# A two-layer spectral and cosine convolution on one core: sums over q as plain transposes with the DFT at their eviction, and one of the shifted inputs copied on chip

## The chip, the cores and the metric

The kernel runs on one core of a Trainium2 chip. The metric is the device time of one execution in microseconds; the time before is 19604.93 us, the median of three (19579.76 to 19606.49). The profiled execution took 19570.94 us.

## The reference

The input x is 4 images of 512 x 512 positions with 16 channels, in fp32. Two residual layers follow each other:

```python
H_truncated = rfft2(b) / rfft2(a)            # b: numerators, a: denominators, 9 x 9 taps
H = rfft2(irfft2(H_truncated), s=(1024, 1024))
X = rfft2(gn(x), s=(1024, 1024))
Y = einsum('...hwi,ijhw->...hwj', X, h0 + H)
x = x + irfft2(Y)[..., :512, :512, :]
# second layer: a 3 x 3 cosine convolution with arccos and tanh of norms
x = x + cosine_conv(gn(x))
```

gn is a group normalization with 8 groups. What matters here is the line with einsum: at each of 513 x 1024 frequencies, 16 input channels are mixed to 16 output channels by a complex 16 x 16 matrix, for four images.

## The kernel before, in words

The work has four phases, one after another: the filter's transform (filter_phase, results to g_d in DRAM), the input's transform along one axis (forward_phase, to x_d), the convolution (conv_phase, from g_d and x_d to y_d), and the inverse transform with the second layer (last_phase). Only conv_phase and its tables are touched by the change.

conv_phase (line 657) goes over 513 rows, one for each frequency of the axis that is already transformed, the first two of which are halves of one stored row. For each row it transforms x along the other axis, multiplies by the filter, and transforms back. The loop is a software pipeline written by hand: `step(n)` (line 849) works on five rows at once, in four quarters k = 0 to 3. A scheduler then orders each engine's instructions by readiness in its own estimate, so an instruction can stand earlier in an engine's stream than in the source. These are the parts, by the tile names that the profile uses:

- `load_x` (705), `turn_x` (716), `x_part` (724): row n+2 of x is transformed by four matmuls with dfs_n, a table turned by this row's own phase (`own`, one column for each row). The result px (PSUM, two banks) is evicted into slot 0 of the tile xe, in two halves.
- `x_late` (739): xe has eight slots, t = 0 to 7. Slot t is slot 0 moved by t places along the spatial axis, that is by 16 t partitions. What moves in from the far end is the same data times a phase; GpSimd computes it as xl, with four products xu (line 753), one product xl (754) and one sum (755). Two stores (746) put slot 0 and xl one below the other into xf_d in DRAM.
- `load_xe` (760): in the next step one load on the sync engine's queue reads seven overlapping windows of xf_d into slots 1 to 7, 3.5 MiB.
- `load_g` (693), `g_part` (768): the filter of row n+1 is loaded to g and transformed with dg: 32 matmuls, pg, evicted to gh.
- `mix` (785): the product at each of 128 frequencies f, 128 matmuls of 32 columns, pm, evicted to yf.
- `over_q` (805): one half of the transform back, over q, for row n-1. yf holds, for a time slot t, partitions (q, c, j) by columns (g, x): q is one of 4 frequency classes, c real or imaginary, j the channel. A matmul with the table iq does two things at once: it puts (g, x) on the partitions, and it sums over q with a phase for each s0 of 4. Sixteen matmuls per row, in groups of four: pz, evicted to z.
- `over_g` (821): the other half, over the 32 values of g, for row n-2: eight matmuls with ig, py, evicted to yo and stored to y_d by GpSimd.

`evict` (line 686) sends copies out of PSUM to VectorE and ScalarE in turn. PSUM has eight banks: three for pg, two for pm, and three, with the tag "full", shared by px, pz and py. xe has three buffers, g, x, gh, yf, z and yo have two, xu and xl have one. The sync engine's queue issues the loads of xe, g and x; GpSimd's queue issues the stores to xf_d and y_d. The step that a reader needs most is the order:

```python
        if row(3):
            load_x(n + 3)
        if row(2):
            load_g(n + 2)
        if row(1):
            load_xe(n + 1)
        for k in range(4):
            ... # mix(n), g_part(n + 1), over_q(n - 1): a quarter each
            if row(2) and k == 0:
                for m in range(B):
                    x_part(n + 2, m)
                x_late(n + 2)
```

Of the kernel before, what the change touches and what calls it, by code (L numbers as in the profile page):

```python
# [40 lines left out]
F32 = mybir.dt.float32  # L41
AF = mybir.ActivationFunctionType
ALU = mybir.AluOpType
# [3 lines left out]
P = 128  # L47
N = 512
B = 4
C = 16  # L50
S = 64
F = 128
# [4 lines left out]
XF = F * 2 * B  # L57
# [12 lines left out]
def constants():  # L70

    c = {}
# [31 lines left out]
    for r in range(33):  # L104
        full = np.zeros((2, S), complex)
# [4 lines left out]
        for part in range(2):  # L110
# [6 lines left out]
            else:  # L117
                v = -(sig.real @ np.sin(f_all))
# [21 lines left out]
    c["own"] = np.tile(own.reshape(-1), (P, 1))  # L140
# [4 lines left out]
    def turn(n, of):  # L145
        a = 2 * np.pi * (n % of) / of
        return np.cos(a), np.sin(a)

    f, sb = np.arange(F), np.arange(S)
    d = np.zeros((2, S, F, 2))  # L150
    co, si = turn(np.outer(sb, f), F)
    d[0, :, :, 0], d[0, :, :, 1] = co, -si
    d[1, :, :, 0], d[1, :, :, 1] = si, co
    c["dfs"] = np.stack([d, np.stack([d[..., 1], -d[..., 0]], -1)], 2).reshape(P, -1)
    co, si = turn(f, F)
    c["late"] = np.tile(np.concatenate([co, si, -si]), (P, 1))

    q1 = np.zeros((4, 2, C, 4, 2, C))
    for q in range(4):
        for cg in range(2):  # L160
            for s0 in range(4):
                co, si = turn(np.array(cg + q * (s0 - 31.5)), 4)
                for j in range(C):
                    q1[q, cg, j, s0, 0, j], q1[q, cg, j, s0, 1, j] = co, si
    c["iq"] = q1.reshape(P, P)

    gg, s1 = np.arange(32), np.arange(16)
    ig = np.zeros((32, 2, 2, 4, 2, 2, 2, 16))
    for s0 in range(4):
        for cx in range(2):  # L170
            for c2 in range(2):
                n = gg[:, None] * (s0 - 31.5) + 4 * gg[:, None] * s1[None, :] + 32 * (cx + c2)
                co, si = turn(n, F)
                for b2 in range(2):
                    ig[:, cx, b2, s0, c2, 0, b2, :] = co / F
                    ig[:, cx, b2, s0, c2, 1, b2, :] = si / F
# [480 lines left out]
def conv_phase(tc, cst, g_d, x_d, y_d):  # L657
    nc = tc.nc
    with ExitStack() as ctx:
# [12 lines left out]
        own = load_const(nc, cp, cst, "own").rearrange("p (v n) -> p v n", v=2)  # L672
        dg = load_const(nc, cp, cst, "dg")
        iq = load_const(nc, cp, cst, "iq")
# [10 lines left out]

        def evict(dst, src):
            flip[0] += 1
            if flip[0] % 2:
                nc.vector.tensor_copy(dst, src)  # L689
            else:  # L690
                nc.scalar.copy(dst, src)  # L691
# [23 lines left out]

        def turn_x(n):

            t = xlp.tile([P, 2 * F], F32, name="turn")
            nc.scalar.activation(t, dfs[:, 1], AF.Identity, scale=own[:, 1, n : n + 1])
            m = xlp.tile([P, 2 * F], F32, name="dfs_n", bufs=2)  # L720
            nc.vector.scalar_tensor_tensor(m, dfs[:, 0], own[:, 0, n : n + 1], t, ALU.mult, ALU.add)
            state["dfs", n] = m

        def x_part(n, b):
# [14 lines left out]
        def x_late(n):  # L739

            xe = state["xe", n][:, 0]
            fl = xe.rearrange("p f h c k -> p f (h c k)")

            def store(half, t):
                at = slice(C, P) if half == 0 else slice(0, P - C)
                nc.gpsimd.dma_start(out=xf_d[n % 4][half * P :, :][at], in_=t[at].rearrange("p f x -> p (f x)"))

            store(0, fl)
            xl = xlp.tile([P, F, 2, 2, 2], F32, name="xl")
            u = xlp.tile([P, F, 2, 2, 2], F32, name="xu")  # L750
            for c in range(2):
                for h in range(2):
                    nc.gpsimd.tensor_mul(u[:, :, h, c], xe[:, :, h, 1 - c], bc(late[:, 1 + c], 2, [P, F, 2]))  # L753
            nc.gpsimd.tensor_mul(xl.rearrange("p f h c k -> p f (h c k)"), fl, bc(late[:, 0], 2, [P, F, 8]))
            nc.gpsimd.tensor_add(xl.rearrange("p f h c k -> p (f h c k)"),
                                 xl.rearrange("p f h c k -> p (f h c k)"),
                                 u.rearrange("p f h c k -> p (f h c k)"))
            store(1, xl.rearrange("p f h c k -> p f (h c k)"))

        def load_xe(n):  # L760
            src = xf_d[n % 4]
            nc.sync.dma_start(
                out=state["xe", n][:, 1:].rearrange("p t f h c k -> p t (f h c k)"),
                in_=bass.AP(tensor=src.tensor, offset=src.offset + C * XF,
                            ap=[[XF, P], [C * XF, 7], [1, XF]]),
            )

        def g_part(n, j):

# [34 lines left out]

        def over_q(n, t):

            y, k = state["y", n], t // 4
            if t % 4 == 0:
                state["pz"] = ps_f.tile([P, 4, P], F32, name="pz", tag="full")
            pz = state["pz"]  # L810
            at = 2 * (2 * k + 1 - t % 4 // 2) + t % 2
            nc.tensor.matmul(pz[:, t % 4], y[:, at].rearrange("p g x -> p (g x)"), iq, start=True, stop=True)  # L812
            if t == 3:
                state["z", n] = yp.tile([P, 8, 2, 8, C], F32, name="z")
            if t % 4 == 3:
                evict(state["z", n][:, 6 - 2 * k : 8 - 2 * k].rearrange("p t h x j -> p (t h x j)"),
                      pz.rearrange("p t x -> p (t x)"))
            if t == 15:
                del state["y", n]

        def over_g(n, k):

            rc, r, plane = rows[n]
            if k == 0:
                state["py"] = ps_f.tile([P, 2, 2, 8, C], F32, name="py", tag="full")
            z, py = state["z", n], state["py"]
            odd, c2 = k // 2, k % 2
            for half in range(2):
                s0 = 2 * half + odd
                nc.tensor.matmul(  # L830
                    py[64 * half : 64 * half + 64, odd], ig[:, s0, c2],
                    z[:, :, :, 2 * s0 + c2, :].rearrange("p t h j -> p h t j"),
                    start=(c2 == 0), stop=(c2 == 1),
                )
            if k < 3:
                return
            del state["z", n]
            yo = yop.tile([P, 4 * P], F32, name="yo")
            evict(yo.rearrange("p (x j t) -> p x j t", x=4, j=C), py.rearrange("p o h t j -> p (o h) j t"))
            if plane is None:  # L840
                nc.gpsimd.dma_start(out=dram(y_d[rc], r, 0, [4 * P, P], [1, 4 * P]), in_=yo)
            else:
                for half in range(2):
                    nc.gpsimd.dma_start(
                        out=dram(y_d[rc], r, (64 * half + 32 * plane) * 4 * P, [4 * P, 32], [1, 4 * P]),
                        in_=yo[64 * half : 64 * half + 32],
                    )

        def step(n):


            def row(k):
                return 0 <= n + k < n_rows
# [8 lines that stand above are left out]
                if row(0):  # L862
                    for g in range(8):
                        mix(n, 8 * k + g)
                if row(1):
                    for j in range(4):
                        g_part(n + 1, 4 * k + j)
                if row(-1):
                    for t in range(4):
                        over_q(n - 1, 4 * k + t)  # L870
                if row(2) and k == 0:
                    for m in range(B):
                        x_part(n + 2, m)
# [452 lines left out]
```

## Time and profile before

The span of the profiled execution, 19569.2 us, divides by the first and last matmul of `mix`:

| stretch, us | phase | length | PE busy | DVE busy | ACT busy | POOL busy | DMA share | GB/s |
|---|---|---|---|---|---|---|---|---|
| 0 to 6980 | filter, then forward | 6980 | 6493.88 | 4826.35 | 3411.00 | 4448.79 | 0.55 | 157 |
| 6980 to 16570 | convolution | 9590 | 8810.89 | 3771.26 | 3061.07 | 4464.24 | 0.88 | 331 |
| 16570 to 19569 | last | 2999 | 2698.54 | 1644.63 | 1553.13 | 1353.38 | 0.52 | 181 |

PE is TensorE's matmul, DVE is VectorE, ACT is ScalarE, POOL is GpSimd and SP the sync engine. In lines of the profile, `pz<-c_iq,yf` is the tile written and the tiles read; a name after `<-` in brackets or after an idle time is what released the instruction. A letter q behind an engine is its instruction queue: SPq issues transfers. An fp32 matmul appears as two instructions. The costliest groups of the convolution, per instruction: pg 288 ns (32832 of them), pm 221 ns (131328), pz 295 ns (16416) on TensorE; 692 ns for a 512-column eviction on VectorE and 586 ns on ScalarE; 718 ns for one xu on GpSimd. These durations include the time in TensorE's pipeline, so that the spacing of their starts, not their sum, tells how long they occupy it.

### The profile page before, as it was taken

Reading aid. Unit: us, or ns where it says so; the run is one execution under the profiler, and the core shown is the slowest. Engines: PE = TensorE matmul, PEld = TensorE weight load, DVE = VectorE, ACT = ScalarE, POOL = GpSimd, SP = SyncE. Lnnn points to the kernel's source line nnn. Section 1 sums busy time; section 2 is a strip of 40 time slices with the busy share of each in tenths; the row PEclk is TensorE's granted clock in tenths of the full one; section 3 lists DMA queues with packets and bytes.
Section 4 is the critical chain, followed back from the end, with each engine's and each line's share of the span. In section 5 each row is a group of like instructions: output and inputs, shape, how many; then the busy total and the mean of one; then the engine's idle time right before and its main releaser. Section 6 shows DMA issues by size and latency. Waiting matters only on the chain. (4 is left out here: it accounts for less than half of the span.)

```text
span 19569.2 us, 539471 instructions
## 1 busy us (share of the span) xinstructions
PE 18003.3 (92%) x235228; PEld 13539.4 (69%) x235228; DVE 10242.2 (52%) x16010; ACT 8025.2 (41%) x14536; POOL 10266.4 (52%) x11419
## 2 busy tenths in 40 slices
PE   8899999999989989999999999999999998988999
PEld 5455555555544467777777777777777776877888
DVE  8877777777753333333333333333333333246656
ACT  4455555555542223333333333333333332106777
POOL 7677777777741134444444444444444443026655
PEclk8899999999999999999999999999999999998999
DMA  3655554555566578888888888888888887796421
GB/s 104 202 149 150 148 142 140 150 148 148 148 195 187 177 288 333 331 332 330 334 331 334 329 334 332 333 331 332 331 334 332 334 331 292 270 325 223 140 74 61
DMA packets 2974924, 4812.42 MB, mean 246 GB/s; under 512 B 109107, under 2 KB 2076813, under 8 KB 2865679
## 3 DMA queue, kind: packets, MB, share of 16 engines
q1 hardware_dynamic: 2742366, 4037.77, 60.1%
q0 software_dynamic: 174896, 605.89, 7.8%
q10 hardware_dynamic: 55296, 134.24, 2.0%
q8 instruction: 1849, 30.29, 0.6%
q14 instruction: 517, 4.23, 0.1%
HBM read 3300.13 MB, written 1477.31 MB: 244 GB/s over the span
## 5 line engine op out<-in xcount | busy, mean ns | idle before, releaser
L753 POOL TENSOR_TENSOR xu<-xe,c_late 128x256 f32<-128x256 f32 x2052 | 1427.6, 718 | 4162.1 <-DVE xe L689 2218.4
L776 PE MATMUL pg<-c_dg,g 64*128 64x128 f32 x32832 | 2477.5, 288 | 437.1 <-DMA g<-g_d 293.1
L689 DVE COPY gh<-pg 128x512 f32<-128x512 f32 x2052 | 1419.4, 692 | 2417.0 <-PE pg L776 2412.6
L792 PE MATMUL pm<-xe,gh 128*32 128x64 f32 x131328 | 2375.8, 221 | 330.6 <-issue 282.2
L792 PEld LDWEIGHTS pm<-xe,gh 128*32 128x32 f32 x131328 | 1983.7, 110 | 877.8 <-issue 725.5
L379 PE MATMUL pg<-c_dinv,sp 128*128 128x256 f32 x8192 | 2278.1, 426 | 295.7 <-ACT st L384 193.1
L776 PEld LDWEIGHTS pg<-c_dg,g 64*128 64x128 f32 x32832 | 2063.4, 190 | 671.7 <-issue 396.6
L812 PE MATMUL pz<-c_iq,yf 128*128 128x128 f32 x16416 | 2465.7, 295 | 27.2 <-issue 21.2
L379 PEld LDWEIGHTS pg<-c_dinv,sp 128*128 128x128 f32 x8192 | 1611.2, 207 | 941.7 <-ACT st L384 217.5
L812 PEld LDWEIGHTS pz<-c_iq,yf 128*128 128x128 f32 x16416 | 2059.4, 197 | 287.7 <-issue 41.2
L691 ACT COPY gh<-pg 128x512 f32<-128x512 f32 x2052 | 1201.7, 586 | 2475.3 <-PE pg L776 2475.2
L355 DVE RECIPROCAL dn<-dn 128x256 f32<-128x256 f32 x1024 | 1790.3, 1748 | 778.8 <-POOL dn L348 778.8
L424 PE MATMUL pt<-ev_in,c_todd 128*128 128x512 f32 x4096 | 1980.2, 609 | 48.5 <-DMA ev_in<-g_d 25.7
L342 ACT COPY ab<-pab 128x512 f32<-128x512 f32 x2048 | 1103.5, 591 | 1136.1 <-POOL m L362 312.3
L689 DVE COPY yf<-pm 128x512 f32<-128x512 f32 x1029 | 711.8, 692 | 1606.4 <-PE pm L792 1584.4
L384 ACT COPY st<-pg 128x256 f32<-128x256 f32 x2048 | 1070.5, 622 | 1019.1 <-PE pg L379 638.3
L1179 PE MATMUL pc<-l_band,xn 128*128 128x160 f32 (+3 forms) x9024 | 1369.3, 308 | 63.3 <-DVE e_o L1226 62.4
L357 POOL TENSOR_TENSOR x<-ab,ab 128x256 f32<-128x256 f32 x1024 | 876.1, 856 | 945.7 <-ACT ab L342 919.4
L1179 PEld LDWEIGHTS pc<-l_band,xn 128*128 128x128 f32 x9024 | 1215.1, 197 | 220.6 <-issue 145.1
L336 PEld LDWEIGHTS pab<-c_e,u 18*128 18x128 f32 x8192 | 722.9, 188 | 809.7 <-ACT st L384 454.2
L424 PEld LDWEIGHTS pt<-ev_in,c_todd 128*128 128x128 f32 x4096 | 812.1, 199 | 676.6 <-issue 520.0
L691 ACT COPY yf<-pm 128x512 f32<-128x512 f32 x1023 | 593.9, 581 | 1578.1 <-PE pm L792 1578.1
(185 smaller groups left out, 28650.5 us busy)
## 6 DMA issues: line engine op xcount, KB each, us to landing
xe<-xf_d SPq DMA_DIRECT2D x513, 3584.0 KB, 14.3
g<-g_d SPq DMA_DIRECT2D x511, 1024.0 KB, 17.0
g_d<-st SPq DMA_DIRECT2D x64, 4096.0 KB, 34.5
ev_in<-g_d SPq DMA_DIRECT2D x1024, 256.0 KB, 4.7
g_d<-ot SPq DMA_DIRECT2D x1024, 256.0 KB, 2.7
xf_d<-xe POOLq DMA_DIRECT2D x513, 448.0 KB, 8.4
xf_d<-xl POOLq DMA_DIRECT2D x513, 448.0 KB, 7.0
x_d<-xo SPq DMA_DIRECT2D x128, 1024.0 KB, 5.4
```

The costliest lines, as they stand in the source:

```text
L342: nc.scalar.copy(w["ab"][n], pp[n])
L355: nc.vector.reciprocal(w["dn"], w["dn"])
L379: nc.tensor.matmul(pg[:, k].rearrange("p a x -> p (a x)"), w["sp"][:, k, c, :], dinv[:, 2 * kp + k, c, :], start=(c == 0), stop=(c == 1),)
L384: nc.scalar.copy(st[a][:, :, i].rearrange("p (q k x) -> p k q x", q=2, k=4)[:, 2 * kp : 2 * kp + 2], pg[:, :, a].rearrange("p k (q x) -> p ...
L424: nc.tensor.matmul(pt, todd[:, c, kc, hh * P : hh * P + P], ev[:, kc, c], start=(kc == 0), stop=(kc == 1),)
L689: nc.vector.tensor_copy(dst, src)
L691: nc.scalar.copy(dst, src)
L753: nc.gpsimd.tensor_mul(u[:, :, h, c], xe[:, :, h, 1 - c], bc(late[:, 1 + c], 2, [P, F, 2]))
L776: nc.tensor.matmul(pg[c][:, j % 4], g[half, j], dg[half], start=True, stop=True)
L792: nc.tensor.matmul(pm[32 * q : 32 * q + 32, g % 8], gh[:, f].rearrange("p c j -> p (c j)"), xe[:, :, f].rearrange("p t h c k -> p t (h c k ...
L812: nc.tensor.matmul(pz[:, t % 4], y[:, at].rearrange("p g x -> p (g x)"), iq, start=True, stop=True)
L1179: nc.tensor.matmul(pc[:, lo:hi, :].rearrange("p w j -> p (w j)"), xns[q][:, h * P + dh : h * P + dh + P], bands[dh][:, o : o + hi - lo, :] ...
```

## The change

It does three things in conv_phase.

First, the sums over q no longer are matmuls with the table iq. `over_q` transposes yf with the identity, which is one instruction instead of two, and the four-point DFT over q is done while pz is evicted: ScalarE copies one half of pz to a tile zq, and VectorE makes sums and differences of it with the other half in five operations, the last ones into z. For odd s0 a product with the imaginary unit is left; GpSimd does it for the whole row with one difference, into a new tile zd, and one sum, in place in z. `over_g` then reads z or zd. For this to be a plain DFT, the offset of 31.5 places is moved from the tables iq and ig into the table dfs.

Second, slot 4 of xe, the input moved by 64 partitions, is not loaded any more. Its lower half is the upper half of slot 0, and its upper half the lower half of xl; ScalarE copies both on chip (`half_shift`). The load of xe becomes two loads of three slots each.

Third, to make room, the table own is loaded in nine pieces as needed, and one eviction in three goes to VectorE, the others to ScalarE, since VectorE has the new work.

```diff
@@ constants
-    co, si = turn(np.outer(sb, f), F)
+    co, si = turn(np.outer(sb + 31.5, f), F)
...
-                n = gg[:, None] * (s0 - 31.5) + 4 * gg[:, None] * s1[None, :] + 32 * (cx + c2)
+                n = gg[:, None] * s0 + 4 * gg[:, None] * s1[None, :] + 32 * (cx + c2)
@@ evict
-            if flip[0] % 2:
+            if flip[0] % 3 == 0:
                 nc.vector.tensor_copy(dst, src)
@@ turn_x
+            for k in range(2) if n == 0 else [n // 64 + 1] if n % 64 == 0 else []:
+                if k < 9:
+                    state["own", k] = xlp.tile([P, 2, 64], F32, name="own", bufs=3)
...
@@ after x_late
+        def half_shift(n, half):
+
+            dst, src = ((slice(0, 64), state["xe", n][64:, 0]), (slice(64, P), state["xl"][:64]))[half]
+            nc.scalar.copy(state["xe", n][dst, 4].rearrange("p f h c k -> p (f h c k)"),
+                           src.rearrange("p f h c k -> p (f h c k)"))
@@ load_xe
-            nc.sync.dma_start(
-                out=state["xe", n][:, 1:].rearrange("p t f h c k -> p t (f h c k)"),
-                in_=bass.AP(tensor=src.tensor, offset=src.offset + C * XF,
-                            ap=[[XF, P], [C * XF, 7], [1, XF]]),
-            )
+            for t in (1, 5):
+                nc.sync.dma_start(
+                    out=state["xe", n][:, t : t + 3].rearrange("p t f h c k -> p t (f h c k)"),
+                    in_=bass.AP(tensor=src.tensor, offset=src.offset + t * C * XF,
+                                ap=[[XF, P], [C * XF, 3], [1, XF]]),
+                )
@@ over_q
-            nc.tensor.matmul(pz[:, t % 4], y[:, at].rearrange("p g x -> p (g x)"), iq, start=True, stop=True)
+            nc.tensor.transpose(pz[:, t % 4].rearrange("p v q x -> p (v q x)"),
+                                y[:, at].rearrange("p g x -> p (g x)"), ident)
...
-                evict(state["z", n][:, 6 - 2 * k : 8 - 2 * k].rearrange("p t h x j -> p (t h x j)"),
-                      pz.rearrange("p t x -> p (t x)"))
+                z = state["z", n][:, 12 - 4 * k : 16 - 4 * k].rearrange("p t (v q) j -> p t v (q j)", v=4)
+                lo = xlp.tile([P, 4, 2, 2 * C], F32, name="zq", bufs=2)
+                nc.scalar.copy(lo, pz[:, :, 0])
+                nc.vector.tensor_sub(z[:, :, 2:4], lo, pz[:, :, 1])
+                nc.vector.tensor_add(lo[:, :, 0], lo[:, :, 0], pz[:, :, 1, 0])
+                nc.vector.tensor_add(pz[:, :, 1, 1], lo[:, :, 1], pz[:, :, 1, 1])
+                nc.vector.tensor_add(z[:, :, 0], lo[:, :, 0], pz[:, :, 1, 1])
+                nc.vector.tensor_sub(z[:, :, 1], lo[:, :, 0], pz[:, :, 1, 1])
             if t == 15:
+
+                z, d = state["z", n], xlp.tile([P, 16, 2, C], F32, name="zd")
+                nc.gpsimd.tensor_sub(d, z[:, :, 4:6], z[:, :, 6:8][:, :, ::-1])
+
+                nc.gpsimd.tensor_add(z[:, :, 4:6], z[:, :, 4:6], z[:, :, 6:8][:, :, ::-1])
@@ over_g
+                if s0 % 2 == 0:
+                    zs = z[:, :, s0 + c2]
+                elif s0 == 1:
+                    zs = (d[:, :, 0], z[:, :, 5])[c2]
+                else:
+                    zs = (z[:, :, 4], d[:, :, 1])[c2]
@@ step, in quarter k
+                if row(2) and k >= 2:
+                    half_shift(n + 2, k - 2)
```

More of the change, by code (lines that the diff above doesn't have):

```diff
@@ L139, in constants @@
     own = np.stack([np.r_[1, -1, np.cos(own)], np.r_[0, 0, np.sin(own)]])
-    c["own"] = np.tile(own.reshape(-1), (P, 1))
+    own = np.pad(own, ((0, 0), (0, 9 * 64 - own.shape[1]))).reshape(2, 9, 64)
+    c["own"] = np.tile(own.transpose(1, 0, 2).reshape(-1), (P, 1))
     inv = fwd * np.where(f > 0, 2.0, 1.0)[:, None] / (2 * N)
@@ L156, in constants @@
     c["late"] = np.tile(np.concatenate([co, si, -si]), (P, 1))
[L158 to L165, printed above, removed]
     gg, s1 = np.arange(32), np.arange(16)
@@ L671, in conv_phase @@
         dfs = load_const(nc, cp, cst, "dfs").rearrange("p (v n) -> p v n", v=2)
-        own = load_const(nc, cp, cst, "own").rearrange("p (v n) -> p v n", v=2)
         dg = load_const(nc, cp, cst, "dg")
-        iq = load_const(nc, cp, cst, "iq")
+        ident = load_const(nc, cp, cst, "ident")
         ig = load_const(nc, cp, cst, "ig").rearrange("p (s c n) -> p s c n", s=4, c=2)
@@ L716, in turn_x @@
         def turn_x(n):
+            for k in range(2) if n == 0 else [n // 64 + 1] if n % 64 == 0 else []:
+                if k < 9:
+                    state["own", k] = xlp.tile([P, 2, 64], F32, name="own", bufs=3)
+                    nc.sync.dma_start(
+                        out=state["own", k].rearrange("p v n -> p (v n)"), in_=cst["own"][:, 128 * k : 128 * k + 128]
+                    )
+            own, at = state["own", n // 64], slice(n % 64, n % 64 + 1)
             t = xlp.tile([P, 2 * F], F32, name="turn")
-            nc.scalar.activation(t, dfs[:, 1], AF.Identity, scale=own[:, 1, n : n + 1])
+            nc.scalar.activation(t, dfs[:, 1], AF.Identity, scale=own[:, 1, at])
             m = xlp.tile([P, 2 * F], F32, name="dfs_n", bufs=2)
-            nc.vector.scalar_tensor_tensor(m, dfs[:, 0], own[:, 0, n : n + 1], t, ALU.mult, ALU.add)
+            nc.vector.scalar_tensor_tensor(m, dfs[:, 0], own[:, 0, at], t, ALU.mult, ALU.add)
             state["dfs", n] = m
@@ L758, in x_late @@
             store(1, xl.rearrange("p f h c k -> p f (h c k)"))
+            state["xl"] = xl
+        def half_shift(n, half):
+            dst, src = ((slice(0, 64), state["xe", n][64:, 0]), (slice(64, P), state["xl"][:64]))[half]
+            nc.scalar.copy(state["xe", n][dst, 4].rearrange("p f h c k -> p (f h c k)"),
+                           src.rearrange("p f h c k -> p (f h c k)"))
         def load_xe(n):
             src = xf_d[n % 4]
-            nc.sync.dma_start(
-                out=state["xe", n][:, 1:].rearrange("p t f h c k -> p t (f h c k)"),
-                in_=bass.AP(tensor=src.tensor, offset=src.offset + C * XF,
-                            ap=[[XF, P], [C * XF, 7], [1, XF]]),
-            )
+            for t in (1, 5):
+                nc.sync.dma_start(
+                    out=state["xe", n][:, t : t + 3].rearrange("p t f h c k -> p t (f h c k)"),
+                    in_=bass.AP(tensor=src.tensor, offset=src.offset + t * C * XF,
+                                ap=[[XF, P], [C * XF, 3], [1, XF]]),
+                )
         def g_part(n, j):
@@ L808, in over_q @@
             if t % 4 == 0:
-                state["pz"] = ps_f.tile([P, 4, P], F32, name="pz", tag="full")
+                state["pz"] = ps_f.tile([P, 4, 2, 2, 2 * C], F32, name="pz", tag="full")
             pz = state["pz"]
             at = 2 * (2 * k + 1 - t % 4 // 2) + t % 2
-            nc.tensor.matmul(pz[:, t % 4], y[:, at].rearrange("p g x -> p (g x)"), iq, start=True, stop=True)
+            nc.tensor.transpose(pz[:, t % 4].rearrange("p v q x -> p (v q x)"),
+                                y[:, at].rearrange("p g x -> p (g x)"), ident)
             if t == 3:
-                state["z", n] = yp.tile([P, 8, 2, 8, C], F32, name="z")
+                state["z", n] = yp.tile([P, 16, 8, C], F32, name="z")
             if t % 4 == 3:
-                evict(state["z", n][:, 6 - 2 * k : 8 - 2 * k].rearrange("p t h x j -> p (t h x j)"),
-                      pz.rearrange("p t x -> p (t x)"))
+                z = state["z", n][:, 12 - 4 * k : 16 - 4 * k].rearrange("p t (v q) j -> p t v (q j)", v=4)
[6 more added lines that the diff above has]
+                nc.vector.tensor_sub(z[:, :, 1], lo[:, :, 0], pz[:, :, 1, 1])
             if t == 15:
+                z, d = state["z", n], xlp.tile([P, 16, 2, C], F32, name="zd")
+                nc.gpsimd.tensor_sub(d, z[:, :, 4:6], z[:, :, 6:8][:, :, ::-1])
+                nc.gpsimd.tensor_add(z[:, :, 4:6], z[:, :, 4:6], z[:, :, 6:8][:, :, ::-1])
+                state["zd", n] = d
                 del state["y", n]
@@ L825, in over_g @@
                 state["py"] = ps_f.tile([P, 2, 2, 8, C], F32, name="py", tag="full")
-            z, py = state["z", n], state["py"]
+            z, d, py = state["z", n], state["zd", n], state["py"]
             odd, c2 = k // 2, k % 2
@@ L829, in over_g @@
                 s0 = 2 * half + odd
+                if s0 % 2 == 0:
[4 more added lines that the diff above has]
+                    zs = (z[:, :, 4], d[:, :, 1])[c2]
                 nc.tensor.matmul(
                     py[64 * half : 64 * half + 64, odd], ig[:, s0, c2],
-                    z[:, :, :, 2 * s0 + c2, :].rearrange("p t h j -> p h t j"),
+                    zs.rearrange("p (t h) j -> p h t j", h=2),
                     start=(c2 == 0), stop=(c2 == 1),
@@ L836, in over_g @@
                 return
-            del state["z", n]
+            del state["z", n], state["zd", n]
             yo = yop.tile([P, 4 * P], F32, name="yo")
```

## The prediction

> **What bounds the kernel now.** First the page's busy line and its forty slices.
>
> ```profile
> PE 18003.3 (92%) x235228; PEld 13539.4 (69%) x235228; DVE 10242.2 (52%) x16010; ACT 8025.2 (41%) x14536; POOL 10266.4 (52%) x11419
> ...
> DMA  3655554555566578888888888888888887796421
> ```
>
> TensorE at 92% looks like the bound, but the convolution, slices 14 to 33, also keeps the DMA engines at 88%. By the view of line 792 its first matmul starts at 6982.3 us and its last at 16568.6: 9586.3 us for 512 steps, 18.72 us a step. Next, the waits between 9000 and 10000 us (53.4 steps).
>
> ```profile
> POOL xu L753 <- DVE xe L689: 233.5, 27, 13.0
> ...
> PE pg L776 <- DMA g<-g_d: 32.2, 27, 2.6
> ```
>
> The DMA queue's own waits in the same stretch:
>
> ```profile
> SPq L762 <- DMA xf_d<-xe: 445.7, 46, 14.0
> SPq L762 <- DMA xf_d<-xl: 301.0, 52, 14.9
> ```
>
> The queue that reloads xe waits 14 us of every step for the two stores to xf_d. TensorE's wait for g is small but comes once per step. The DMA view of 9500 to 9600 us (2.5 us a slice) shows one hole per step:
>
> ```profile
> DMA  9939999993699999728999994499999918999996
> ```
>
> The timeline gives the order. TensorE:
>
> ```profile
> 9561.89 1.16 PE L776 MATMUL pg<-c_dg,g 64*128 64x128 f32 x16 [0.82 <-DMA g<-g_d]
> 9562.99 1.16 PE L812 MATMUL pz<-c_iq,yf 128*128 128x128 f32 x8
> 9563.98 1.89 PE L732 MATMUL px<-dfs_n,x 128*128 128x256 f32 x8
> ```
>
> GpSimd:
>
> ```profile
> 9565.89 1.53 POOL L753 TENSOR_TENSOR xu<-xe,c_late 128x256 f32<-128x256 f32 x2 [7.98 <-DVE xe L689]
> ...
> 9573.95 0.58 POOL L746 DMA_DIRECT2D xf_d<-xl  x1 [0.29 <-POOL xl L755]
> ```
>
> The queue:
>
> ```profile
> 9543.35 0.37 SPq L762 DMA_DIRECT2D xe<-xf_d  x1
> ...
> 9581.62 0.37 SPq L762 DMA_DIRECT2D xe<-xf_d  x1
> ```
>
> This is a ring. The load of xe, with g behind it, is issued at 9543.35; g lets TensorE go on at 9561.89 (18.54 us later); px starts at 9563.98 (2.09); its eviction releases GpSimd at 9565.89 (1.91); the second store is issued at 9573.95 (8.06); it lands and the reload of two steps later goes out at 9581.62 (7.67). The sum, 38.27 us, is two steps. Averaged over the timeline's steps from 7500 to 16000 us whose landings are recorded, the terms are 17.62 (xe issue to g landed), 2.93, 1.98, 8.07 and 6.69, with 0.08 to the issue: 37.37 us, 18.69 a step against 18.72. So the kernel is bound by this ring of transfers. TensorE without waits needs, by the spacing of the starts in the same timeline, four times 1.03 (pm) + 1.09 (pg) + 1.07 (pz), with px 1.82 and py 1.88: 16.5 us. It waits 2.2 us a step although it counts as busy.
>
> [...]
>
> **The change part by part.**
>
> *Transposes.* 16 fp32 matmuls a step are two instructions each (16416 is 32 per step); a group of four takes 1.09 us from start to start, 0.99 ahead of px. The transposes of line 1101 and line 613 are one instruction each, and four take 0.45 us in the timeline of the forward phase (6006.84 to 6007.29). I take 0.50 for the switch. TensorE saves 4 x 0.57 = 2.3 us: 14.2 us a step of its own. Of this only the group between pg and px, 0.5 us, lies on the ring.
>
> *Less to load, in two pieces around g.* Seven slots of 512 KB become six, 3 ahead of g and 3 behind (the built program has this order; x goes ahead of them). The last wanted is now the second half of xe, after 4.0 MiB instead of 4.5. Loading g takes 17.62 - 14.46 (xe's average landing) = 3.2 us for 1.0 MiB, so 0.5 MiB less is 1.6: 16.0 us from issue to the last landing. But xe is wanted by the first pm, g only by the pg behind it: 1.03 us more follow the landing.
>
> *Landing to px.* 1.03 (pm) + 1.09 (pg) + 0.50 (pz) + 0.1 to start = 2.7 us (2.93 before).
>
> *px to GpSimd.* ScalarE now always takes the first half of xe. Where it did before, 9507.76 to 9509.53, it took 1.77 us; the copy of pz ahead of it (0.4 us) is over by then.
>
> *GpSimd to the second store.* 8.07 us, plus a wait: VectorE's half of xe, which the first store needs, stands behind five new operations. [...] It starts 0.8 after px does, so VectorE's xe is over at 3.3, and GpSimd would have been ready at 1.77 + 1.35 = 3.1. I add 0.3: 8.4 us. If an operation costs 400 ns, it is 0.8 us.
>
> *The two new GpSimd operations* (512 elements each) stand ahead of xu. Line 1217 takes 1.28 us for 512, so 2.6 together. They are free only if they end before xe is ready. Their start depends on the last pz group of the step, and this on ScalarE's copies of half of xe: the built program puts the second of these, which waits for xl, behind the second pz copy of the step and not at the end. It will hold ScalarE's queue: behind it stand a yf, a gh, a pz copy and yo, and TensorE's fourth pg group waits for that gh's buffer. Counted from xu's start: xl ready 8.1; copy 1.1 (509 ns for 256 elements at line 719 and 710 for 512 at line 1205 give 0.79 ns an element; 617 for 512 at line 1196 give 1.02 for 1024): 9.2; yf and gh at 0.5 each: 10.2; pg 1.1 and pz 0.7: 12.0; pz copy 0.5; VectorE 1.75; GpSimd 2.6: 16.9 us, when xu of the next step could start. That is a second ring of one step, 16.9 us, with 16.2 to 18.3 for slower or quicker pieces. Below the first, it hides.
>
> *Stores.* 6.69 us before, of which about 5.7 lay beside the loads and 1.0 after them. The loads end sooner, so the store has the engines alone longer: between 4.4 (the least landing in the view of line 746 from 9000 to 10000 us) and 6.7; I take 6.3.
>
> *Others, at nothing.* ScalarE has 10 evictions, 4 copies of pz, 2 half copies and one turn: 10 x 0.585 + 4 x 0.42 + 2 x 1.02 + 0.51 = 10.1 us a step, VectorE 5 x 0.69 + 4 x 1.75 + 0.85 = 11.3, GpSimd 8.7 + 2.6 = 11.3: all under 17, and the rings hold what of them is on the path. The own table comes in 9 small loads, two pieces ahead. over_g reads other strides of the same bytes. The other phases are the same.
>
> Sum: 16.0 + 2.7 + 1.8 + 8.4 + 6.3 + 0.1 = 35.3 us in two steps, 17.65 a step; I take 17.7 because the second ring is close. Saved: (18.72 - 17.7) x 512 = 520 us, 19604.9 - 520 = 19085, said as 19090. With the bounds: store 4.4 and no added wait gives 16.5, where the second ring holds it at 16.9 or more; store 7.2, the added wait 0.8, landing 16.6 gives 18.3.
>
> **The rivals.** *TensorE was the bound.* For it: 92%. Against it: the ring's sum and the hole. Then the saving is 2.3 x 512 = 1180: 18430 us. *Half the gain is eaten*: the second ring at 18.3 sets the step, 215 us saved, 19390. *Slower*: with z operations of 0.4 us (2.1 a group)[...], and a store no faster, the zd pair ends 2 us after xe is ready, is added to the first ring once per step, and TensorE, which now waits about 3.5 us a step, drops its clock as it did at 9542.51 (pg 2.03 us instead of 1.16), right on the ring. Ring one gets 35.3 + 0.4 + 2 + 1.6 (half clock on a part of pm, pg, px) = 39.3, 19.65 a step: 480 us more, 20080. For it: three engines' queues are newly tied together. Against it: each has 6 us of slack a step.
>
> **How the numbers follow.** Forecast, 18700 to 19350: 0.55. Half eaten, 19350 to 19565: 0.17. TensorE bound or a much quicker store, under 18700: 0.08. No change within 0.2% (39 us): 0.06. Slower: 0.14. Faster is 0.55 + 0.17 + 0.08 = 0.80. The range 18700 to 19600 leaves out 0.08 below and about 0.13 above.
>
> **What would show it.** Right: about 17.7 us a step; TensorE's wait once a step is for xe and not for g; the queue still waits for xf_d; one hole per step in the DMA line; ScalarE waiting on GpSimd's xl some 3 us a step; pz's rows halved in count. Wrong: xu released by zd instead of xe (the second ring rules); TensorE without any wait (it was the bound); a granted clock in the convolution clearly under its 0.98; a DMA line without holes.

## The result, and the profile after

The kernel after takes 19064.0 us (median of 4 runs, 19048.82 to 19086.82) against 19605.71 us before (4 runs, 19579.76 to 19609.93): ratio 0.9727, 95% interval 0.9711 to 0.9744, or 542 us less. The page of the kernel after, its busy line and the DMA row of its forty slices:

```profile
PE 17293.1 (91%) x227020; PEld 12605.2 (66%) x227020; DVE 11398.8 (60%) x23961; ACT 9747.4 (51%) x17871; POOL 11564.3 (61%) x12445
...
DMA  3755455555557668888888888888888887796321
```

Neither line tells that anything became faster: TensorE is at 91% instead of 92%, the DMA engines are as full as before (0.87 of the convolution against 0.88). Only the convolution is shorter. Its first pm matmul (line 799 now) starts at 6990.1 us, its last at 16042.0: 9051.9 us for 512 steps, **17.68 us a step** against 18.72. The phases ahead of it and behind it take as long as before, within 10 us each.

The waits of the kernel after between 9000 and 10000 us, 56.6 steps (total us, times, longest):

```profile
ACT xe L763 <- POOL xl L754: 208.1, 57, 6.5
...
POOL xu L752 <- ACT xe L683: 93.6, 56, 6.9
```

ScalarE waits for GpSimd's xl 3.7 us a step, as it must for the second half copy. GpSimd's xu still waits for xe, not for zd: the new GpSimd operations are over in time. TensorE's own waits in the same stretch:

```profile
PE pm L799 <- issue: 41.6, 45, 2.9
PE pg L783 <- issue: 18.0, 13, 3.2
PE pg L783 <- ACT gh L683: 16.1, 21, 2.5
PE pm L799 <- DMA xe<-xf_d: 14.0, 10, 2.9
```

Its wait for g is gone and one for xe has come, but only in 10 steps of 57. The largest item, "issue", is a stop for which the profile shows no cause; the experiments will come back to it. The DMA queue's waits, and the DMA row from 9500 to 9600 us (2.5 us a slice), which still has one hole per step:

```profile
SPq L769 <- DMA xf_d<-xl: 724.7, 56, 14.5
```

```profile
DMA  9995799999539999974998995599999539999964
```

The timeline of the kernel after, one turn of the ring (start, length, engine, line; the bracket is the idle time ahead and who ended it):

```profile
9509.52 0.37 SPq L769 DMA_DIRECT2D xe<-xf_d  x1
...
9530.33 1.89 PE L731 MATMUL px<-dfs_n,x 128*128 128x256 f32 x8
...
9532.07 1.37 POOL L752 TENSOR_TENSOR xu<-xe,c_late 128x256 f32<-128x256 f32 x2 [1.28 <-ACT xe L683]
...
9540.15 0.58 POOL L745 DMA_DIRECT2D xf_d<-xl  x1 [0.29 <-POOL xl L754]
...
9545.05 0.37 SPq L769 DMA_DIRECT2D xe<-xf_d  x1
```

From load to load it is 35.53 us, two steps, as before but 2.7 us shorter. Averaged over the 190 turns between 7500 and 15500 us whose landings are recorded:

| term, us | predicted | after |
|---|---|---|
| issue of xe to its last landing | 16.0 | 15.78 |
| landing to px | 2.7 | 4.22 |
| px to xu | 1.8 | 1.75 |
| xu to the second store | 8.4 | 8.13 |
| store's landing | 6.3 | 5.31 |
| to the next issue | 0.1 | 0.16 |
| sum, two steps | 35.3 | 35.36 |

The sum is met to 0.1 us, but that alone shows little: the terms run from one issue to the issue two steps later, so in any kernel they add up to two steps, whatever binds it. A ring binds only where each piece starts as soon as the one before it ends. Two terms are off by 1.5 and 1.0 us against each other, and "landing to px" is 1.5 us over its tenth percentile (2.75), which is what it takes when nothing else holds px. With 2.75 the ring would need 33.9 us, 16.9 a step. So the ring has slack there, and something else is about as slow. The experiments look for it.

### The profile page after: what moved, and what is told of

Read it like the earlier page. It is cut to its first block, busy times and chain, and to the rows that moved or that the text cites. A ratio compares the mean times of both kernels' runs of the same rounds, so it can differ in the third digit from the quotient of the medians.

```text
span 19052.5 us, 536690 instructions
## 1 busy us (share of the span) xinstructions
PE 17293.1 (91%) x227020; PEld 12605.2 (66%) x227020; DVE 11398.8 (60%) x23961; ACT 9747.4 (51%) x17871; POOL 11564.3 (61%) x12445
## 5 line engine op out<-in xcount | busy, mean ns | idle before, releaser
L783 PE MATMUL pg<-c_dg,g 64*128 64x128 f32 x32832 | 2842.9, 291 | 320.9 <-ACT gh L683 159.5
L783 PEld LDWEIGHTS pg<-c_dg,g 64*128 64x128 f32 x32832 | 2283.2, 190 | 662.7 <-issue 262.5
L828 DVE TENSOR_TENSOR z<-zq,pz 128x256 f32<-128x256 f32 x2052 | 862.0, 420 | 2617.2 <-ACT zq L827 2534.6
L683 ACT COPY yf<-pm 128x512 f32<-128x512 f32 x2046 | 1210.5, 592 | 919.0 <-PE pm L799 904.3
L763 ACT COPY xe<-xl 64x1024 f32<-64x1024 f32 x513 | 538.8, 1050 | 1877.0 <-POOL xl L754 1877.0
L820 PE MATMUL pz<-c_ident,yf 128*128 128x128 f32 x8208 | 1378.2, 291 | 27.2 <-issue 25.4
```

What stands on the lines that cost most here:

```text
L783: nc.tensor.matmul(pg[c][:, j % 4], g[half, j], dg[half], start=True, stop=True)
L820: nc.tensor.transpose(pz[:, t % 4].rearrange("p v q x -> p (v q x)"), y[:, at].rearrange("p g x -> p (g x)"), ident)
```

## The experiments

The theory is the prediction's: a ring of fixed terms through the transfers sets the step. The rivals are that the one-step ring through ScalarE's half copy does, that the bytes to be moved do, or that TensorE does. Ratios are to the kernel before, measured beside each.

### One part of the change alone

transposes_only keeps the change but for the copies; shift_only has only the copies.

Of transposes_only, against after:

```diff
-            for t in (1, 5):
-                nc.sync.dma_start(
-                    out=state["xe", n][:, t : t + 3].rearrange("p t f h c k -> p t (f h c k)"),
...
+            nc.sync.dma_start(
+                out=state["xe", n][:, 1:].rearrange("p t f h c k -> p t (f h c k)"),
...
-                if row(2) and k >= 2:
-                    half_shift(n + 2, k - 2)
```

shift_only makes the same edit the other way round in the kernel before, with `half_shift` added.

> The kernel after with its transposes and its new evictions, but the seven slots of xe loaded in one piece and no copies on the chip. If the ring of transfers sets the step, it loses only the 0.6 us of one pz group in two steps: 18.4 us a step, 160 us under the kernel before. If TensorE alone was the bound, 2.3 us a step: 1180 us under it.

> The kernel before with six slots loaded in two pieces and the two half copies, but the sums over q still as fp32 matmuls. If the ring of transfers alone sets the step, 35.3 + 0.6 us in two steps, 17.95 a step: 400 us under the kernel before. If TensorE, with its stops under load, needs about 18.4 us a step with the old matmuls (where the kernel before without the GpSimd sum ended), it can't fall below that: 160 us under. If the bytes loaded set it, 8% of 18.7 us: 700 us under.

transposes_only: 19624.14 us, ratio 1.0016 (1.0010 to 1.0023). shift_only: 19182.33 us, ratio 0.9794 (0.9780 to 0.9809), 416 us less. So the transposes alone bring nothing, the copies alone three quarters of the 542 us that both bring together: the transposes are worth some 120 us, but only once the copies are there.

The first is a miss of 0.3 us a step for the ring. Why it gained nothing, its waits and timeline show:

```profile
PE pg L782 <- DMA g<-g_d: 79.5, 34, 5.6
```

```profile
9531.42 0.76 PE L782 MATMUL pg<-c_dg,g 64*128 64x128 f32 x2 [5.59 <-DMA g<-g_d]
...
9532.12 1.93 PE L798 MATMUL pm<-xe,gh 128*32 128x64 f32 x64
...
9533.98 2.07 PE L782 MATMUL pg<-c_dg,g 64*128 64x128 f32 x14
...
9535.98 1.11 PE L819 MATMUL pz<-c_ident,yf 128*128 128x128 f32 x4
```

TensorE, quicker by the transposes, now waits 79.5 us instead of 32.2 for g. But the way from g's landing to px, which is on the ring, takes 4.23 us on average against 3.15 in the kernel before. Two things lengthen it. First, TensorE's instructions stand in another order: between the pg that waits for g and px there is now a group of pm, as these lines show, where the kernel before had pg and pz alone. Even the tenth percentile of this way is 3.13 us instead of 2.22, though pz is shorter. Second, after the idle time of 5.59 us TensorE runs at half its clock (granted 0.50 over these lines): pm 1.93 us instead of 1.10, pg 2.07 instead of 1.16, pz 1.11 instead of 0.66. Of the 266 steps between 7500 and 15500 us whose landing is recorded, the clock stays over 0.98 between g and px in 150, and the way takes 3.52 us; in 112 it is under 0.9, and the way takes 5.08. Together they eat what the shorter pz saves there.

shift_only agrees with the fixed ring (17.95 a step; measured 17.92). Yet its TensorE doesn't wait for data at all; its stops are of this kind:

```profile
9525.44 0.92 PE L784 MATMUL pg<-c_dg,g 64*128 64x128 f32 x5 [2.32 <-issue]
9526.29 2.07 PE L820 MATMUL pz<-c_iq,yf 128*128 128x128 f32 x8
```

So its agreement is no proof of the ring: TensorE itself set this one (a table below has 17.0 us busy and 0.8 us of stops in its 17.9). After this stop of 2.32 us pz takes 2.07 us instead of 1.16, nearly twice as long.

### Shortening GpSimd's part of the ring

before_no_sum leaves out the sum of xl and xu in the kernel before (its output misses that term).

```diff
-            nc.gpsimd.tensor_add(xl.rearrange("p f h c k -> p f (h c k)"),
-                                 xl.rearrange("p f h c k -> p f (h c k)"),
-                                 u.rearrange("p f h c k -> p f (h c k)"))
```

> The kernel before, with GpSimd's sum into xl (line 755, 2.36 us a step) left out, so that the late half of the input is only its first product. Nothing of TensorE's work changes. If the kernel before is bound by its ring of transfers, which goes through GpSimd once in two steps, the ring's 37.4 us become 37.4 - 2.4 = 35.0, 17.5 a step instead of 18.72: 1.2 x 512 = 610 us less, about 18990 us. If TensorE at 92% were the bound, the time would stay at 19600.

It took 19434.27 us, ratio 0.9916 (0.9896 to 0.9935). The way from xu to the second store fell from 8.03 to 5.60 us, 1.2 us a step, but the step only by 0.26 (18.72 to 18.46). The store's landing stretched from 6.72 to 7.83 us and the way from g to px from 3.15 to 3.47. TensorE's waits in it:

```profile
PE pm L789 <- issue: 33.8, 45, 1.8
PE pg L773 <- issue: 22.8, 21, 2.2
PE pg L773 <- DMA g<-g_d: 14.6, 16, 2.0
```

The wait for g has halved, and "issue" is the greater part. So the ring held the kernel before, but something else, by these waits TensorE, stood only some 0.3 us a step behind it.

### ScalarE's wait, and the product on VectorE

hs_end places the half copy of xl behind the step's last pz copy; hs_end_dve also moves the product of xl from GpSimd to VectorE.

```diff
-                nc.scalar.copy(lo, pz[:, :, 0])
+                state["last"] = nc.scalar.copy(lo, pz[:, :, 0])
...
-                if row(2) and k >= 2:
-                    half_shift(n + 2, k - 2)
+                if row(2) and k == 2:
+                    half_shift(n + 2, 0)
+                if row(2) and k == 3:
+                    if row(-1):
+                        with tc.issue_after(state["last"].ins):
+                            half_shift(n + 2, 1)
...
```

hs_end_dve, besides:

```diff
-            nc.gpsimd.tensor_mul(xl.rearrange("p f h c k -> p f (h c k)"), fl, bc(late[:, 0], 2, [P, F, 8]))
+            nc.vector.tensor_mul(xl.rearrange("p f h c k -> p f (h c k)"), fl, bc(late[:, 0], 2, [P, F, 8]))
```

> The changed kernel, with ScalarE's copy of xl into slot 4 put behind the last copy of pz of the step, where xl has long been ready, instead of behind the second. If ScalarE's 3.7 us of waiting for xl close the ring that binds, they go, and the ring of transfers is left: its 35.4 us less the 1.5 us by which px now comes later than the landing needs, 33.9, or 16.9 a step: 390 us less, about 18670. If the ring of transfers binds already, or TensorE does, nothing is gained: 19064 within 60 us.

> As the one before, and the first product of xl (line 753, 1.98 us) moved from GpSimd to VectorE, which has some 5 us a step to spare. [...] GpSimd's way from px to the second store gets 2.0 us shorter, so if the ring of transfers binds once ScalarE's wait is gone, 1.0 us a step more is saved: 15.9 a step, held by TensorE's own 15.4 plus its stops at about 16.2: 18300 us. If the move of the half copy already left TensorE as the bound, it gives nothing beyond that kernel[...].

hs_end: 19068.65 us, ratio 0.9734 (0.9717 to 0.9750), no gain over after. hs_end_dve: 19033.22 us, ratio 0.9708 (0.9694 to 0.9723), no gain that these runs can tell. In hs_end TensorE waits for the load of xe 23 times in 56 steps (45.1 us between 9000 and 10000 us, against 14.0 in the kernel after), so the ring of transfers takes the place of ScalarE's wait. One such step:

```profile
9545.02 1.10 PE L799 MATMUL pm<-xe,gh 128*32 128x64 f32 x64 [3.55 <-DMA xe<-xf_d]
9546.05 1.77 PE L783 MATMUL pg<-c_dg,g 64*128 64x128 f32 x14
9547.76 1.11 PE L820 MATMUL pz<-c_ident,yf 128*128 128x128 f32 x4
9548.67 2.47 PE L731 MATMUL px<-dfs_n,x 128*128 128x256 f32 x8
```

Again the half clock after a long wait lies on the ring (0.55 granted from 9546.1 to 9549 us). In hs_end_dve the product takes 1.27 us on VectorE, against 1.98 on GpSimd, the way from xu to the store is 1.3 us shorter, and TensorE's waits are:

```profile
PE pm L799 <- issue: 75.4, 62, 4.2
PE pg L783 <- issue: 18.3, 14, 3.6
PE pg L783 <- DMA g<-g_d: 6.5, 2, 3.7
```

Now TensorE hardly waits for data, so both rings have slack, and almost all of TensorE's idle time is "issue", 1.7 us a step by these two lines. Something other than data stops it.

### Fewer transfers, and transfers that nobody reads

half_loaded is after without the second load of xe; the matmuls of pm read slots 0 to 3 twice instead of 0 to 7, so the output is another. half_hs_dve is hs_end_dve with the same cut. unread_dve makes both loads, but reads slots 0 to 3 twice all the same.

The first edit is in half_loaded and half_hs_dve, the second in all three:

```diff
-            for t in (1, 5):
+            for t in (1,):
...
-                    xe[:, :, f].rearrange("p t h c k -> p t (h c k)"), start=True, stop=True,
+                    xe[:, 0:4, f].rearrange("p t h c k -> p t (h c k)").unsqueeze(1).to_broadcast([P, 2, 4, 8]),
+                    start=True, stop=True,
```

> The changed kernel, with the second of the two loads of xe left out and the product reading slots 0 to 3 twice, so that half of the shifted inputs are wrong. Each step loads 1.5 MiB less; all instructions on TensorE, VectorE, ScalarE and GpSimd stay. If the ring of transfers still binds the changed kernel, it loses the 5.2 us between the landing of g (10.5 us after the issue) and that of the second load (15.8), 2.6 us a step, and the time falls until TensorE's own 15.5 us a step or another limit stops it: 17900 to 18000 us. If the changed kernel is bound by a one-step ring instead, from px over ScalarE's copy, GpSimd's xl, ScalarE's half copy and the gh behind it to TensorE's next pg, pz and px, no transfer is on it and the time stays within 150 us of 19064 (somewhat less only because fewer transfers stand beside the others).

> Computes something else: the second load of xe is left out, slots 0 to 3 are read twice; besides, the half copy stands last and VectorE makes the product of xl. Transfers and ScalarE's wait are both out of the way, so TensorE's own need is left: its busy time of 15.5 us with stops of about 0.7: 16.2 us a step, 18300 us. If some ring through GpSimd binds instead, it stays at the 17.0 us a step and 18718 us that the half loads alone gave.

> Computes something else: half_hs_dve, but with the second load of xe made and not read, so that TensorE waits for as little as there and the transfers are those of hs_end_dve. If the wait for the second piece was what the half loads took away, 15.8 us a step, 18110 us, as half_hs_dve. If it is the traffic itself, through TensorE's stops and the ring's landings, 17.6 us a step, 19033, as hs_end_dve.

half_loaded: 18718.42 us, ratio 0.9550 (0.9531 to 0.9569), between the two values expected. TensorE no longer waits for any load. But ScalarE's wait for xl is still there, and TensorE waits for the gh that stands behind it:

```profile
ACT xe L763 <- POOL xl L754: 206.9, 59, 6.5
...
PEld pg L783 <- ACT gh L683: 36.9, 39, 4.0
```

With that wait gone too, half_hs_dve takes 18110.73 us, ratio 0.9240 (0.9226 to 0.9254), 15.85 us a step. So the one-step ring through GpSimd's xl and ScalarE is real, at some 17.05 us a step where nothing else holds, 0.6 us below the kernel after. half_hs_dve moves the copy and the product at once; what each brings is not split. In the kernel after it ran beside the other ring, and removing it alone (hs_end) brought nothing.

unread_dve takes 18996.16 us, ratio 0.9703 (0.9688 to 0.9717): as slow as hs_end_dve, though no matmul reads what the second load brings. The stretch from 8000 to 15000 us, first of unread_dve and then of half_hs_dve (the last three figures are TensorE's granted clock, the DMA engines' busy share, GB/s):

```profile
8000.00:15000.00 7000.00, 6247.52 (x142947) 4997.69 (x142949) 4308.05 (x10720) 3832.80 (x6751) 3925.74 (x3971) 0.97 0.86 323
```

```profile
8000.00:15000.00 7000.00, 6713.51 (x158928) 5410.75 (x158920) 4772.99 (x11918) 4276.39 (x7506) 4371.07 (x4414) 1.00 0.72 260
```

The traffic itself slows TensorE: 17.6 us a step with the unread load, 15.85 without it. How, the DMA view of unread_dve from 9000 to 10000 us shows in one row (packets, MB, share):

```profile
q8 instruction: 160, 2.62, 1.0%
```

That is 16 KB a packet. In unread_dve's 7000 us there are 1121 of them and 285896 records of matmuls and weight loads, 255 for each packet. In hs_end_dve, with 1120 such packets, TensorE is idle for more than 0.25 us 570 times in these 7000 us, and 517 of those stops end between 1.1 and 1.7 us after the end of an instruction packet (median 1.40; by chance it would be one in ten), one stop for about every second packet. From this it is read that TensorE stops for want of instructions; the profile itself names no cause. That the packets come late because the DMA engines are loaded is argued from the next comparison; a packet's own transfer takes a median 0.96 us in unread_dve and in half_hs_dve alike. Taking stops that end so as fetches, and idle time over 0.15 us as waits, TensorE's step is (8000 to 15000 us, scaled to the step):

| kernel | us a step | TensorE busy | fetch stops | other waits |
|---|---|---|---|---|
| before | 18.7 | 17.2 | 0.9 | 0.6 |
| before_no_sum | 18.5 | 17.1 | 1.0 | 0.4 |
| shift_only | 17.9 | 17.0 | 0.8 | 0.1 |
| transposes_only | 18.8 | 16.1 | 1.1 | 1.6 |
| after | 17.7 | 15.9 | 1.2 | 0.6 |
| hs_end_dve | 17.7 | 15.8 | 1.6 | 0.3 |
| unread_dve | 17.6 | 15.7 | 1.6 | 0.3 |
| half_hs_dve | 15.85 | 15.2 | 0.6 | 0.0 |

Unread traffic makes 1.0 us of stops a step, and 0.5 us more busy time at a lower clock. The 0.3 us that are left are the other waits.

### Moving less: slot 2 copied on chip as well

copies24 is hs_end with slot 2 of xe copied like slot 4, in four copies of 32 rows, three of them on VectorE; slots 1, 3, 5, 7 and 6 are loaded, 0.5 MiB less. copies24_act has all copies on ScalarE; copies24_bal besides gives every second eviction and the product of xl to VectorE.

```diff
...
+                if row(2) and k == 1:
+                    shift(n + 2, 2, 0, 32, nc.scalar.copy)
+                    shift(n + 2, 2, 32, 32, nc.vector.tensor_copy)
+                if row(2) and k == 2:
+                    shift(n + 2, 4, 0, 64, nc.scalar.copy)
+                    shift(n + 2, 2, 64, 32, nc.vector.tensor_copy)
+                if row(2) and k == 3:
+                    with tc.issue_after(state["last"].ins) if row(-1) else ExitStack():
+                        shift(n + 2, 4, 64, 64, nc.scalar.copy)
+                        shift(n + 2, 2, 96, 32, nc.vector.tensor_copy)
...
```

copies24_act has `nc.scalar.copy` in all six; copies24_bal, besides:

```diff
-            if flip[0] % 3 == 0:
+            if flip[0] % 2 == 0:
...
-            nc.gpsimd.tensor_mul(xl.rearrange("p f h c k -> p f (h c k)"), fl, bc(late[:, 0], 2, [P, F, 8]))
+            nc.vector.tensor_mul(xl.rearrange("p f h c k -> p f (h c k)"), fl, bc(late[:, 0], 2, [P, F, 8]))
```

> Slots 2 and 4 of xe are both copied on the chip (six copies a step, four on ScalarE's and VectorE's way in the middle of the step, two last), slots 1, 3, 5, 7 and 6 are loaded: 0.5 MiB less a step than after. If the transfers' bytes set the step, 8 to 9% of 17.7 us less: 18350 us. If TensorE with its stops sets it, it gains only what lighter traffic takes off the stops, some 0.3 us a step: 18900. If the fuller queues of VectorE and ScalarE hold TensorE's evictions, no gain or slower than 19064.

> The same as copies24, but all six copies on ScalarE. If VectorE's copies of 3.4 us beside GpSimd's operations were what made copies24 slow, they go, and the lighter transfers show: 16.5 to 17.2 us a step, 18450 to 18800. If copying 32 rows out of and into xe costs so much on any engine, or ScalarE, at some 13.5 us a step, holds TensorE's evictions, it stays over 19064.

> copies24_act with every second instead of every third eviction on VectorE (ScalarE some 12.0, VectorE some 12.6 us a step) and the product of xl on VectorE. If full queues limit copies24_act, it is 200 us or more under that; if TensorE with its stops limits both, within 60 us of it.

copies24: 21726.03 us, ratio 1.1088 (1.1072 to 1.1105), far slower than any case expected. Its timeline:

```profile
9520.54 6.88 DVE L764 COPY xe<-xe 32x1024 f32<-32x1024 f32 x2
...
9524.19 2.68 POOL L754 TENSOR_TENSOR xl<-xl,xu 128x1024 f32<-128x1024 f32 x1
...
9527.45 0.69 DVE L681 COPY gh<-pg 128x512 f32<-128x512 f32 x1
...
9528.20 2.07 PE L788 MATMUL pg<-c_dg,g 64*128 64x128 f32 x14 [5.01 <-DVE gh L681]
...
9528.95 0.69 DVE L764 COPY xe<-xl 32x1024 f32<-32x1024 f32 x1
```

Two VectorE copies take 6.88 us and end 0.55 us after GpSimd's last operation does; the third, of the same shape, runs when GpSimd is idle and takes 0.69. Between 8000 and 15000 us the two take 3402 ns each on average, the third 686. The slow ones lie beside GpSimd's tensor-tensor operations, the quick one does not; by what mechanism, no run here shows. Behind the copies stands the eviction of gh, and TensorE stops for 5.01 us in this step (199.1 us in 43 steps between 9000 and 10000 us).

copies24_act: 18733.79 us, ratio 0.9563 (0.9547 to 0.9579), 330 us under after, the best of the kernels that leave nothing out: 17.10 us a step with DMA at 83%. So the engine was the fault, not the copy. Nor do the bytes alone set the step: by the GB/s of 8000 to 15000 us (302 and 322) this kernel moves 9% less a step than after, and its step is 3% shorter. Against hs_end, on which it builds, TensorE's waits fall from 0.6 to 0.2 us a step, reckoned as in the table above; its fetch stops hardly change (1.4 and 1.3). copies24_bal: 18865.48 us, ratio 0.9639 (0.9616 to 0.9662). It is slower, against both expectations. In the same reckoning TensorE's other waits fall from 0.2 to 0.1 us a step, but its fetch stops rise from 1.3 to 1.6 (busy 15.6 and 15.7). So full queues held copies24_act by no more than 0.1 us a step. Why the stops grow, with DMA at 81% instead of 83%, stays open.

## Why the prediction was right, and where its working was not

**The total.** 19064 against 19090; 17.68 us a step against 17.7. The change shortened the ring where the prediction said: the loads land after 15.8 us instead of 17.6 (predicted 16.0), and four of the six terms came within 0.3 us.

**The terms that missed, and the luck in the total.** The landing of the store was sized 6.3 and is 5.31; landing to px was sized 2.7 and is 4.22. The second holds slack and half-clock time: its tenth percentile is 2.75, as sized. So the ring by itself needs 16.9 us a step, not 17.65, and the 0.7 us to the measured step are this slack and half-clock time. Beside the ring stand the one through ScalarE (17.05 in half_loaded) and TensorE with its stops (17.1). That the store's error and the slack cancel for the most part is luck. By these figures the ring of transfers is one of three bounds within 0.2 us of each other, not the one that sets the step; how the three make 17.68 together stays open.

**The second ring.** It was put at 16.9 us, through zd. Up to the half copy the trace follows it: xl ready at 7.8 us from xu (predicted 8.1), copy 1.08 (1.1). But zd ends 1.63 us before xu starts, so the way closes through TensorE instead: the held evictions, then pm, pg, pz, pm, pg and pz to px, 7.0 us, then 1.75 to xu. These pieces, too, add up to the step in any case; how slow this ring is by itself, half_loaded shows: 17.05. The size was right, the path was not.

**VectorE's new work.** The prediction's 1.75 us for a group of five operations, which its second ring and VectorE's sum use, was the author's estimate and not shown by any trace of before. The trace of after has 420 ns for the operation on 256 elements, 280 to 295 for the four on 128, and 1.59 us from the start of the first to the end of the last. The estimate was 0.16 us high, and the way from xu to the store, 8.13 us against 8.07 before, shows that the five operations cost the path almost nothing.

**TensorE.** "14.2 us a step of its own" is the step that failed without costing the total. It was summed from undisturbed spacings: by the timeline a pz group now takes 0.49 to 0.59 us where it took 1.07, so about 2.0 us are saved instead of 2.3. Left out were 1.2 us of fetch stops, and 1.4 us by which the busy time, 15.9, exceeds the 14.5 that are then left; the granted clock of 0.98 makes about 0.3 of that, and the rest is not split. TensorE needs 15.9 + 1.2 = 17.1 us under this traffic, not 14.2, and would have capped any larger gain. The rival "TensorE was the bound" was wrong of the kernel before, but 17.2 + 0.9 = 18.1 us puts it 0.6 under the step, not 2.2. That is why before_no_sum gained so little.

**The transposes.** "Of this only the group between pg and px, 0.5 us, lies on the ring" would make them worth 0.3 us a step alone. They were worth nothing alone: the pm group that came between g and px, and the half clock that the "slower" rival named, ate it. With the copies they bring 0.24 us a step (17.92 to 17.68), since TensorE with the old matmuls needs 17.0 + 0.8 us and would hold the step there.

**Readings and signs that were off.** The ring's sum in the kernel before, 37.37 us, was taken as proof that the ring binds; it is two steps in any case. TensorE's wait for g was read as one in every step, but its line has 27 in 53.4 steps; in the other half g had landed before TensorE came to it, and the ring had slack. The upper bound, with 7.2, 0.8 and 16.6 put into the sum, is 37.3 us or 18.6 a step, not 18.3; nothing came of it. And of the signs of being right, a wait of TensorE for xe once a step came in only 10 of 57.

## What to carry to other kernels

When two or three bounds lie within a few per cent, a term taken off one of them pays only up to the next: work out TensorE's bound with its stops under the real traffic, not from undisturbed spacings. A ring's terms, summed around the ring, give the step whatever binds it; compare them with what each takes when nothing holds it. Unused TensorE time was not free here where it came in one piece of 2 us or more: after 151 of 175 such stops in transposes_only the granted clock fell under 0.75, and some of the matmuls that it slowed stood on the path. With the DMA engines at 86%, bytes cost more than the wait for them: a load that no matmul reads made TensorE's stops for instructions 1.0 us a step longer. Moving less by copying on chip paid in copies24_act, with the copies on ScalarE, where one of 32 rows took 1.05 us beside GpSimd's work (copies24).

## What the runs showed of the hardware that was not expected

- Most of TensorE's stops without a shown cause end 1.1 to 1.7 us after a packet of instructions (517 of 570 in hs_end_dve), of which there is one of 16 KB per 255 records (unread_dve), so they are read as late instruction fetches: 1.6 us of stops a step with the DMA engines at 86%, 0.6 at 72% (unread_dve, half_hs_dve). That they end a median 1.40 us after the packet is shown; that the packet queues behind the loads is argued from the comparison of the two.
- In copies24 a VectorE copy of 32x1024 fp32 takes 0.69 us, and 3.4 us beside GpSimd's tensor-tensor operations; ScalarE's takes 1.05 us there.
- After TensorE was idle for 3.55 or 5.59 us, pg took 1.77 and 2.07 us and px up to 2.47, instead of 1.16 and 1.89. Shorter stops do it too, some of the time. In transposes_only, from 8000 to 15000 us, the granted clock fell under 0.75 within 2 us after 4 of 292 stops of 0.3 to 1.5 us, 22 of 75 of 1.5 to 2 us, 56 of 78 of 2 to 3 us, and 95 of 97 longer ones.
